# A graph network's gated projection: the first quarter split into exact parts, and the attention step ahead of it reordered

## The chip, the core and the metric

The kernel is a hand-written program for one core of a Trainium2 chip. The core has five engines that run side by side: TensorE (PE in the profile; its weight loads are shown apart as PEld), VectorE (DVE), ScalarE (ACT), GpSimd (POOL) and SyncE (SP, which here only issues DMAs). The metric is the time of one execution on the device, in microseconds (us); lower is better. Times are compared as medians of several runs.

## The reference, cut to what matters

1024 nodes with 512 features; 16 graphs of 64 nodes each attend to 256 rows of a condition of their own. Everything is float32.

```python
h = gcn(batch_norm(relu(layernorm(x))))            # dense 1024x1024 adjacency, built from 16384 edges
for i in range(4):
    h = h + attn(ln(h, ln2[i]), cond, Wq[i], Wk[i], Wv[i], Wo[i])   # 8 heads of 64
    u = ln(h, ln3[i]) @ geglu_w[i] + geglu_b[i]    # 512 -> 4096
    val, gate = split(u, 2)                        # 2048 and 2048
    h = h + (val * gelu(gate)) @ ffo_w[i] + ffo_b[i]
out = x + gcn(h) + x_in
```

The change touches the line with `geglu_w` (the gated projection) and the last two of the eight attention steps ahead of it.

## The kernel before

**Products by parts.** Most products are made of three matrix products of reduced operands: each float32 operand is split into a high part, a low part and a third one that joins both, all held in a type that TensorE takes in one pass (`float32r`, F32R). ACT makes the high part by one multiplication, DVE the low part by one `scalar_tensor_tensor`, and DVE or POOL the third. A unit of the class `Twelve` multiplies high by high and low by low into one PSUM bank (`begin`), lets ACT scale the bank, adds the product of the thirds (`end`), and an engine copies the bank out. Plain float32 matmuls are used in few places; each shows as two records in the trace.

**The gated projection.** Its output has 2048 value and 2048 gate columns, worked on in 16 column blocks of 128 (value block and gate block together), in four rounds `r` of four blocks `c`. Node and feature dimensions are halved, and the 2x2 blocks are multiplied by seven products in place of eight (a Strassen-Winograd scheme), which needs sums of blocks of the activations (`ln3S`, from `ln3T`) and of the weights. The result of a block column goes through Gelu and a product into `fT`, and by DMA to `f_dram`.

- Round 0 (`r = 0`) is done by four `Quad`s: seven plain float32 products each, of two 128x128x512 matmuls (the helper `multiply`, L304). `geglu_weights` forms the weight sums on POOL. `first` and `second` of each `Quad` (products 0 and 1) are put in between the pieces of the last attention step; `rest` does the other five and calls `fill`, which meanwhile splits the seven activation operands for the later rounds (`begin_right`, `finish_right`, `right_beside`).
- Rounds 1 to 3 are done by twelve `Chunk`s: the same seven products, each by parts, so 42 matmuls (L1121). `Chunk.sums` (POOL) forms the weight sums, `split_steps` splits them (ACT, DVE, POOL), `steps` is the order of the products.

**The attention ahead of it.** There are eight steps `g`, one for each 128 nodes (two graphs). A step makes the next step's keys and values (`keys`, `values`, units of `Twelve`, L379), mixes its own values by the probabilities (`mix`: transposes L205, `weigh` L874, then the three parts of the result, L898 to L902), makes the next step's probabilities (`scores`: L840 on PE; on DVE the row maximum L847, on ACT two exponentials L852, on DVE the reciprocal L855 and two multiplications L857, four times), and adds the projected result to `h` (`attn_out`, L912, DVE L917 and L920). After that, the rows of `h` are normalised (`moments`, `deviations`, `scaled`) and turned into `ln3T` (`ln3_turn`: four transposes, eviction by DVE L825 or ACT L827). `add_bias` (L1583) adds the last bias of the layer to `h` ahead of time.

**What sets the order.** `pin` keeps an instruction in program order among the others so marked. `with in_order(DVE)` chains every DVE instruction of a block to the one before it, in the order in which the block's text issues them; elsewhere a planner orders each queue by priority and expected readiness. Tiles of 128x1024 come from a pool of 35 `slots`; matmuls write to 8 PSUM banks.

Of the kernel before, what the change touches and what calls it, by code (L numbers as in the profile page):

```python
# [26 lines left out]
def gnn_kernel(  # L27
# [205 lines left out]
    def sums_of_b(t, b11, b12, b21, b22, t1, t2, t4, t_last=None):  # L233


        t.tensor_tensor(t1, b12, b11, OP.subtract)
        t.tensor_tensor(b12, b22, b12, OP.subtract)
        t.tensor_tensor(t2, b22, t1, OP.subtract)
        return (t_last or t).tensor_tensor(t4, b21, t2, OP.subtract)

    def sums_of_a(t, a11, a12, a21, a22, s1, s2, s4):

        t.tensor_tensor(s1, a21, a22, OP.add)  # L243
        t.tensor_tensor(a21, a11, a21, OP.subtract)
        t.tensor_tensor(s2, s1, a11, OP.subtract)
        return t.tensor_tensor(s4, a12, s2, OP.subtract)

    def halves_of(t):
        return t.rearrange("p (a b) -> p a b", a=2)

# [44 lines left out]

    def blocks_of_w(w):
        return [w[k][:, :, d * M:(d + 1) * M] for d in range(2) for k in range(2)]

    def multiply(to, left, right, cols_of, start, each=lambda ins: ins):

        for n, (l0, l1, r0, r1) in enumerate(cols_of):
            at = to if len(cols_of) == 1 else to[:, n * (r1 - r0):(n + 1) * (r1 - r0)]
            for k in range(2):
                each(nc.tensor.matmul(at, left[:, k, l0:l1], right[:, k, r0:r1],  # L304
                                      start=start and n == 0 and k == 0,
                                      stop=n == len(cols_of) - 1 and k == 1,
                                      skip_group_check=True))
# [634 lines left out]
    def order7(blk, s1, s2, s4):  # L942

        return [blk[0], blk[1], s4, blk[3], s1, s2, blk[2]]

    def load_geglu(l, r):
        return [load_w(geglu_w[l][:, r * D:(r + 1) * D], f"wval_{l}_{r}"),
                load_w(geglu_w[l][:, DFF + r * D:DFF + (r + 1) * D], f"wgate_{l}_{r}")]

    def geglu_weights(l, r, wval, wgate):  # L950
        s = slots_of(3, f"ges_{l}_{r}")
        sums_of_a(nc.gpsimd, *wval, *wgate, *s)
        return order7([*wval, *wgate], *s)

    class Quad:

        def __init__(self, l, r, c, left, right, f):
            self.n, self.c, self.f = f"{l}_{r}_{c}", c, f  # L960
            self.cv = l * 2 * DFF // P + r * KC + c
            self.left, self.right = left, right

        def product(self, i, to, start, each=lambda ins: ins):
            multiply(to, self.left[i], self.right[i],
                     [(self.c * P, (self.c + 1) * P, 0, 512)], start, each)

        def first(self):
            self.a = bank(f"ga_{self.n}")
            self.product(0, self.a, True)  # L970
            if self.c % 2 == 0:
                Quad.room = slot(f"gs1_{self.n}")
            self.s1 = Quad.room[:, self.c % 2, :]
            nc.scalar.copy(self.s1, self.a)

        def second(self):
            self.product(1, self.a, False)

        def gate(self, pre, name):
            cg = self.cv + DFF // P  # L980
            nc.scalar.activation(pre, pre, AF.Gelu, bias=gcols[:, cg:cg + 1])

        def rest(self, fill):
            n, bias = self.n, gcols[:, self.cv:self.cv + 1]
            b, c, d = (bank(f"{x}_{n}") for x in ("gb", "gc", "gd"))
            u2, u3 = (acc_tile(f"g{x}_{n}") for x in ("u2", "u3"))
            g0, g1 = (t512(f"{x}_{n}") for x in ("g0", "g1"))
            f0, f1 = self.f.of(self.c)

            def add(to, x, y):  # L990
                self.last = pin(nc.vector.tensor_tensor(to, x, y, OP.add))

            self.product(5, b, True, pin)
            add(u2, b, self.s1)
            at_once = self.c in (1, 2)
            if not at_once:
                fill()
            if not self.c:
                fill()
            self.product(6, c, True, pin)  # L1000
            add(u3, c, u2)
            if at_once:
                fill()
            fill()
            self.product(4, d, True, pin)
            add(g1, d, u3)
            self.gate(g1, n)
            fill()
            self.product(3, c, False, pin)
            add(g0, c, u2)  # L1010
            self.gate(g0, n)
            fill()
            self.product(2, d, False, pin)
            add(d, d, u2)
            pin(nc.vector.scalar_tensor_tensor(f0, self.a, bias, g0, OP.add, OP.mult))
            pin(nc.vector.scalar_tensor_tensor(f1, d, bias, g1, OP.add, OP.mult))
            self.f.store(self.c)
            fill()
            fill()

    SPLIT = (0, 5, 6, 4, 1, 3, 2)
    EARLY = (0, 1, 4, 6, 5, 3, 2)
    BESIDE = (4, 6)

    def begin_right(name, x, h, s):

        nc.scalar.mul(h.bitcast(F32R), x, INWARD / TINY)
        for k in range(2):
            more = t512(f"{name}_{k}")
            nc.scalar.mul(more, h[:, k, :], 1.0 + TINY)  # L1030
            yield
            pin(nc.vector.scalar_tensor_tensor(s.bitcast(F32R)[:, k, :], x[:, k, :], 1.0 / TINY,
                                               more, OP.mult, OP.subtract))

    def finish_right(name, x, h):

        low = slot(name)
        for k in range(2):
            yield low
            pin(nc.vector.scalar_tensor_tensor(low.bitcast(F32R)[:, k, :], x[:, k, :], 1.0 / TINY,  # L1040
                                               h[:, k, :], OP.mult, OP.subtract))
# [29 lines left out]
    class Chunk:  # L1071
# [78 lines left out]
        def steps(self, sum_next):  # L1150
# [7 lines left out]
            self.banks = {}  # L1158
            self.scale(0)
            yield  # L1160
            self.scale(5)
            yield
            s1, u2, u3 = (acc_tile(f"g{x}_{n}") for x in ("s1", "u2", "u3"))
            pin(nc.scalar.copy(s1, self.end(0)))
# [27 lines left out]
    class Gated:  # L1192
# [10 lines left out]
        def store(self, c):  # L1203
            for s in range(2):
                nc.sync.dma_start(f_dram[s, self.r * KC + c], self.tiles[c][:, s, :])

    def quads_of(l, r, left, right):
        f = Gated(l, r)
        return f, [Quad(l, r, c, left, right, f) for c in range(KC)]
# [227 lines left out]
    for l in range(L):  # L1437
# [238 lines left out]
        def all_parts():  # L1676
            for i in EARLY:
# [17 lines left out]
                for _ in flow:  # L1695
                    yield
# [275 lines left out]
```

## Time and profile before

| | |
|---|---|
| median of 3 runs | 2288.28 us (2287.64 to 2288.84) |
| profiled execution | 2287.76 us, its span 2286.0 us |
| TensorE busy | 2262.3 us, 99% of the span |
| VectorE busy | 1649.5 us, 72% |
| ScalarE busy | 1125.7 us, 49% |
| GpSimd busy | 587.2 us, 26% |

The span runs from the first to the last instruction; 1.8 us of the execution lie around it. Busy times are averages over stages that differ: the prediction reads the stage of the change by itself. The first layer's stage runs from 353.84 us (first key product of step 6) to 445.30 us (first `Chunk`), and there are four such stages, one a layer.

### The profile page before, as it was taken

To read this page: it belongs to the slowest core of one execution; us is meant where nothing else is said; L and a number is where in the kernel's file an instruction comes from. 1 tells how busy PE (TensorE), PEld (TensorE's weight loads), DVE (VectorE), ACT (ScalarE), POOL (GpSimd) and SP (SyncE) were. 2 spreads that over 40 slices of the span, in tenths; PEclk is the share of its full clock that TensorE was granted. 3 is DMA by queue.
4 is the path that set the end of the run, shared out by engine and by line. 5 is a ranking of instruction groups with operands and counts; after the bars stand their busy time and mean duration, and the time that the engine had idled before them with its cause. 6 is when DMAs were issued, how large, how long until landed. Compare 5 with 4: busy or idle time off the path is not lost. (4 is left out here: it accounts for less than half of the span.)

```text
span 2286.0 us, 34523 instructions
## 1 busy us (share of the span) xinstructions
PE 2262.3 (99%) x12496; PEld 1754.6 (77%) x12496; DVE 1649.5 (72%) x3124; ACT 1125.7 (49%) x2197; POOL 587.2 (26%) x551
## 2 busy tenths in 40 slices
PE   8999999999999999999999999999999999999999
PEld 4678887587888888488888888578888888668787
DVE  9876556999965445989976444989976444899965
ACT  7555545565354445465345444655436444556521
POOL 1121213485000002377000001368100000368301
PEclk9999999999999999999999999999999999999999
DMA  5154331234425331133534242133543332043551
GB/s 170 57 184 167 148 116 60 83 120 147 170 81 183 125 111 42 61 117 100 194 120 170 94 139 70 37 111 102 184 157 134 125 116 97 1 129 111 178 182 56
DMA packets 162545, 271.54 MB, mean 119 GB/s; under 512 B 13288, under 2 KB 70960, under 8 KB 162368
## 3 DMA queue, kind: packets, MB, share of 16 engines
q1 hardware_dynamic: 160272, 263.83, 33.7%
q0 software_dynamic: 1376, 4.30, 0.6%
q8 instruction: 103, 1.69, 0.3%
q10 hardware_dynamic: 720, 1.11, 0.1%
q14 instruction: 74, 0.61, 0.1%
HBM read 202.08 MB, written 67.11 MB: 118 GB/s over the span
## 5 line engine op out<-in xcount | busy, mean ns | idle before, releaser
L1135 ACT ACTIVATE g<-g 128x512 f32<-128x512 f32 x192 | 112.4, 586 | 153.2 <-PE g L1121 151.3
L243 POOL TENSOR_TENSOR ges<-wgate,wgate 128x1024 f32<-128x1024 f32 x4 | 9.6, 2393 | 676.6 <-DMA wgate<-in_L_gnn_geglu_w_dram 441.6
L390 ACT ACTIVATE k<-k 128x512 f32<-128x512 f32 x125 | 73.1, 586 | 194.2 <-PE k L379 194.2
L1264 PE MATMUL fx<-bs_wff,as_f 128*128 128x512 f32 x512 | 158.7, 390 | 0.0
L1264 PE MATMUL fy<-bl_wff,al_f 128*128 128x512 f32 x512 | 158.6, 390 | 0.0
L1264 PE MATMUL fy<-bh_wff,ah_f 128*128 128x512 f32 x512 | 157.8, 389 | 0.0
L321 ACT ACTIVATE ah_f<-fr 128x1024 fp32r<-128x1024 f32 x64 | 67.9, 1060 | 179.5 <-DVE al_f L322 79.8
L395 DVE COPY kT<-k 128x512 f32<-128x512 f32 x54 | 37.3, 691 | 159.5 <-PE k L379 159.1
L847 DVE TENSOR_REDUCE nmax<-sc 128x2 f32<-128x512 f32 x128 | 83.0, 679 | 88.2 <-PE sc L840 88.2
L390 ACT ACTIVATE v<-v 128x512 f32<-128x512 f32 x127 | 74.7, 588 | 137.9 <-PE v L379 137.9
L1065 POOL TENSOR_TENSOR gsa<-gha,gla 128x512 fp32r<-128x512 f32 x96 | 124.2, 1317 | 43.7 <-DVE gla L1060 43.7
L852 ACT ACTIVATE pr<-sc,nmax 128x256 f32<-128x256 f32 x256 | 118.1, 474 | 31.7 <-DVE nmax L847 31.1
L1121 PE MATMUL g<-gr,gha 128*128 128x512 f32 x384 | 120.0, 394 | 0.0
L1121 PE MATMUL g<-gr,gsa 128*128 128x512 f32 x384 | 119.8, 393 | 0.0
L1121 PE MATMUL g<-gl,gla 128*128 128x512 f32 x384 | 118.4, 389 | 0.0
L1264 PEld LDWEIGHTS fy<-bl_wff,al_f 128*128 128x128 f32 x512 | 96.1, 188 | 21.6 <-DVE bl_wff L1241 1.6
L1264 PEld LDWEIGHTS fx<-bs_wff,as_f 128*128 128x128 f32 x512 | 96.1, 188 | 21.4 <-DVE bs_wff L1245 1.7
L1264 PEld LDWEIGHTS fy<-bh_wff,ah_f 128*128 128x128 f32 x512 | 96.1, 188 | 19.9
L379 PE MATMUL v<-bh_wv,ch 128*128 128x512 f32 x384 | 106.4, 399 | 0.0
L322 DVE SCALAR_TENSOR_TENSOR al_f<-ah_f,fr 128x1024 fp32r<-128x1024 f32 x64 | 78.1, 1220 | 39.1 <-ACT ah_f L321 33.0
L379 PE MATMUL k<-ch,bh_wk 128*128 128x512 f32 x384 | 103.4, 391 | 0.0
L1312 POOL TENSOR_TENSOR as_wq<-ah_wq,al_wq 128x512 fp32r<-128x512 f32 x16 | 21.1, 1342 | 319.7 <-DVE al_wq L1310 286.2
(333 smaller groups left out, 6015.8 us busy)
## 6 DMA issues: line engine op xcount, KB each, us to landing
f_dram<-fT SPq DMA_DIRECT2D x128, 256.0 KB, 2.1
fr<-f_dram SPq DMA_DIRECT2D x64, 512.0 KB, 5.1
ch<-cond_dram SPq DMA_DIRECT2D x48, 512.0 KB, 4.8
cl<-cond_dram SPq DMA_DIRECT2D x48, 512.0 KB, 6.1
cs<-cond_dram SPq DMA_DIRECT2D x48, 512.0 KB, 7.1
wff<-in_L_gnn_ffo_w_dram SPq DMA_DIRECT2D x32, 512.0 KB, 5.5
gxa<-in_L_gnn_geglu_w_dram SPq DMA_DIRECT2D x96, 128.0 KB, 2.5
gxb<-in_L_gnn_geglu_w_dram SPq DMA_DIRECT2D x96, 128.0 KB, 2.5
```

The costliest lines, as they stand in the source:

```text
L321: nc.scalar.mul(twelve_bits(h), x, INWARD * TINY)
L322: left_parts.low = nc.vector.scalar_tensor_tensor(twelve_bits(l), h, -1.0 / TINY, x, OP.mult, OP.add)
L379: pin(nc.tensor.matmul(self.bank, twelve_bits(left[k // 2])[:, k % 2, self.c * P:(self.c + 1) * P], twelve_bits(right[k // 2])[:, k % 2, : ...
L390: nc.scalar.mul(self.bank, self.bank, 1.0 + TINY)
L395: nc.vector.tensor_copy(self.to(), self.bank)
L847: nc.vector.tensor_reduce(nmax, ps3, AX.X, OP.max, negate=True)
L852: nc.scalar.activation(pr3[:, a, :], ps3[:, a, :], AF.Exp, bias=nmax[:, a:a + 1], accum_out=tot[:, a:a + 1])
L1065: split_left.last = pin(t.tensor_tensor(s_at, h_at, l_at, OP.subtract))
L1121: pin(nc.tensor.matmul(to, self.part(i, which)[:, k, :], self.rights[i][which].bitcast(F32R)[:, k, :], start=start and k == 0, stop=stop a ...
L1135: pin(nc.scalar.mul(to, to, 1.0 + TINY))
L1264: pin(nc.tensor.matmul(to, twelve_bits(left[which][0])[:, k, b * P:(b + 1) * P], twelve_bits(right[which])[:, k, :], start=u == 0 and whic ...
L1312: nc.gpsimd.tensor_tensor(twelve_bits(s)[:, k, :], h[:, k, :], l[:, k, :], OP.subtract)
```

## The change

Round 0 is done in another way, and steps 6 and 7 are written out anew:

- The four `Quad`s and all that served them alone are gone (`geglu_weights`, `multiply`, `begin_right`, `finish_right`).
- Column blocks 0 and 1 of round 0 (`PLAIN = 2`) are done without the seven-product scheme: for each half of the nodes, a gate unit and a value unit a block, each a `Half(Twelve)` of 12 matmuls by parts. Its weights are loaded by two DMAs (`HalfWeights`) and split into parts; its activations are the split blocks 0 and 1 of `ln3T` for the first half, and 7 and 2 for the second.
- Column blocks 2 and 3 become `Chunk`s like those of the later rounds: 14 `Chunk`s a layer, not 12.
- The activation operands are split elsewhere: 0 and 1 within step 6 (third part on POOL), 7 and 2 by column halves within step 7, the sums 5, 6, 4 and 3 beside the second half's units. Operand 7, the unchanged block, is new; `ln3_last_sum` replaces it by its difference later.
- Step 6 is wholly inside one `in_order(DVE)` block, the `scores` of step 7 among it; its `attn_out` moves into step 7, as a hook of `mix` between the transposes and `weigh`. The transposes of normalised blocks move to between the keys. The bias is added by POOL alone.

```diff
+    class Half(Twelve):
...
+        def multiply(self, which, start, stop):
+            for k in range(KC):
+                right = self.right[k // 2][which]
+                pin(nc.tensor.matmul(self.bank, twelve_bits(self.left[which])[:, k, ...],
+                                     twelve_bits(right)[:, k % 2, :], ...))
+        def end(self):
+            self.multiply(2, False, True)
+            self.emit(self.bank)
...
+        take_ln3()
+        weights = HalfWeights(l)
+        load()
+        with in_order(mybir.EngineType.DVE):
+            k = keys(l, g + 1, wk)
+            k[0].begin()
...
+            ln3_turn(0, (1, 1), pin)
+            ln3_turn(1, (0, 0), pin)
+            add_bias(nc.gpsimd, *range(4))
...
+            ln3_norm(g - 2, g - 1)
...
+            oT = mix(l, g, probs, vs.pop(g), (
+                k[-1].end, lambda: split_early(0), v[0].begin,
+                lambda: split_early(1)))
+            add_bias(nc.gpsimd, g - 2, g - 1)
+            weights.split(1)
+            probs = scores(l, g + 1, qT, kTs.pop(g + 1))
+            oT = oT()
+            weights.split(0)
+            v[1].begin()
+            v[0].end()
+            ln3_turn(g - 2, (1, 1), pin)
+            v[2].begin()
+            v[1].end()
+            ln3_turn(g - 1, (0, 0), pin)
+            ln3_sums(nc.gpsimd, g - 2, g - 1)
+            sum_chunk(0)
+            v[3].begin()
+            v[2].end()
...
+        with in_order(mybir.EngineType.DVE):
+            units = half_0(0) + half_0(1)
...
+            oT = mix(l, g, probs, vs[g], (v[3].end, attn_before))
+            units[0].begin()
+            oT = oT()
+            split_late(slice(0, 2 * P))
+            long = begin_split(0, False)
+            next(long)
+            for _ in attn_out(l, g, oT, wo, pin):
+                pass
...
+            units[1].begin()
+            units[0].end()
...
+            units[2].begin()
+            units[1].end()
+            units[3].begin()
+            ln3_turn(g - 1, (1, 1), pin)
+            ln3_turn(g, (0, 0), pin)
+            units[2].end()
+            ready[0].begin_first()
+            units[3].end()
+            split_late(slice(2 * P, 4 * P))
+            ready[0].end_first()
+            ln3_sums(nc.vector, g - 1, g)
+            ln3_last_sum(nc.gpsimd, g - 3, g - 2)
+            ln3_last_sum(nc.gpsimd, g - 1, g)
...
+        units = half_1(0) + half_1(1)
+        units[0].begin()
+        fill(2)
+        units[1].begin()
+        units[0].end()
...
-        for r in range(1, R):
+        for r in range(R):
-            for c in range(KC):
+            for c in range(0 if r else PLAIN, KC):
```

More of the change, by code (lines that the diff above doesn't have):

```diff
@@ L289, in gnn_kernel @@
     left = None
[L296 to L307, printed above, removed]
     def twelve_bits(t):
@@ L940, in out_parts @@
             yield
[L942 to L1019, printed above, removed]
@@ L1770, in split_rest @@
+        for _ in range(2):
+            next(first_flow)
+        fill(2)
+        units[3].end()
+        load()
+        second = begin_split(1, False)
+        add_bias(nc.gpsimd, g - 1, g)
         def split_rest(short, behind=None):
@@ L1812, in gnn_kernel @@
                         next(before, None)
+                    elif not step:
+                        next(second)
                     next(flow)
                     if step == 1 and not before:
-                        split_rest(iter(()))
+                        for _ in second:
+                            pass
+                        sum_chunk(1)
                         load()
```

333 lines of the change are left out of this document (179 added, 154 removed).

## The prediction, made before the changed kernel was run

> **What bounds the kernel now.** I read the page's busy times first, then the busy time of each engine in the four stages of the change (a layer each; the fifth row is the first layer's `Chunk` loop, from another answer of the same view), then TensorE's waits.
>
> ```profile
> PE 2262.3 (99%) x12496; PEld 1754.6 (77%) x12496; DVE 1649.5 (72%) x3124; ACT 1125.7 (49%) x2197; POOL 587.2 (26%) x551
> core 0: us, PE busy (x) PEld busy (x) DVE busy (x) ACT busy (x) POOL busy (x), PEclk, DMA share, GB/s
> 353.84:445.30 91.46, 90.53 (x462) 55.81 (x460) 74.71 (x158) 45.02 (x86) 34.61 (x30) 1.00 0.15 50
> 880.76:972.22 91.46, 90.54 (x462) 55.83 (x460) 74.93 (x158) 45.03 (x86) 34.67 (x30) 1.00 0.15 48
> 1407.84:1499.72 91.88, 90.53 (x462) 55.82 (x460) 75.70 (x158) 45.02 (x86) 34.61 (x30) 1.00 0.16 50
> 1935.33:2026.78 91.45, 90.53 (x462) 55.81 (x460) 74.64 (x158) 45.02 (x86) 34.63 (x30) 1.00 0.15 47
> 445.30:560.00 114.70, 114.70 (x502) 93.42 (x500) 104.55 (x148) 68.84 (x118) 89.30 (x88) 1.00 0.35 111
> PE po L874 <- DVE pT L888: 1.2, 4, 0.3
> ```
>
> TensorE is the bound nearly everywhere, at full clock, and the stages are alike. So the time is TensorE's own work plus what it waits. In the `Chunk` loop it waits for nothing although DVE is busy 91% and POOL 78%: busy helpers alone do not stop it. Only a serial chain that ends later than TensorE arrives does.
>
> **TensorE's work: what goes and what comes.** The first layer's plain products and the pace of both kinds (columns of the last four rows: start, length, then how many):
>
> ```profile
> L304 PE MATMUL ga<-ln3T,wval 128*128 128x512 f32 x32 | 14.8, 595 | 0.0
> L304 PE MATMUL gd<-ln3T,ges 128*128 128x512 f32 x16 | 7.7, 604 | 0.5 <-DVE g L991 0.5
> L304 PE MATMUL gc<-ln3S,wgate 128*128 128x512 f32 x16 | 7.6, 599 | 0.1
> L304 PE MATMUL gc<-ln3T,wgate 128*128 128x512 f32 x16 | 7.5, 592 | 0.0
> L304 PE MATMUL gb<-ln3S,ges 128*128 128x512 f32 x16 | 7.5, 592 | 0.0
> L304 PE MATMUL gd<-ln3S,ges 128*128 128x512 f32 x16 | 7.5, 592 | 0.0
> 437.12 1.88 PE L304 MATMUL gb<-ln3S,ges 128*128 128x512 f32 x4
> ...
> 443.98 1.88 PE L304 MATMUL gd<-ln3T,ges 128*128 128x512 f32 x4
> 356.57 1.07 PE L379 MATMUL k<-ah_c,bh_wk 128*128 128x512 f32 x4
> ...
> 361.11 1.07 PE L379 MATMUL k<-ah_c,bh_wk 128*128 128x512 f32 x4
> 423.86 1.88 PE L304 MATMUL gc<-ln3S,wgate 128*128 128x512 f32 x4
> 426.28 1.98 PE L304 MATMUL gd<-ln3T,ges 128*128 128x512 f32 x4 [0.54 <-DVE g L991]
> 445.30 1.02 PE L1121 MATMUL g<-gr,gha 128*128 128x512 f32 x2
> ```
>
> There are 32 + 5 x 16 = 112 records, four to a product (two matmuls, two records each): 28 products a layer. Matmuls overlap, so the price is the distance of starts: 437.12 to 443.98 is four products, 1.715 us each. The matmuls by parts take (361.11 - 356.57) / 20 = 0.227 us each.
>
> - Removed: 28 x 1.715 = 48.0 us a layer.
> - Added: 2 blocks x 2 halves x 2 (gate, value) x 12 = 96 matmuls, and 2 `Chunk`s x 42 = 84; 180 x 0.227 = 40.9 us. The nearest row, the `Chunk` loop, has no lost time at 12 x 42 matmuls in about 115 us, so I take this pace for both.
> - Moved at the same count: the key, value, `scores`, `mix`, `attn_out` and turning matmuls.
>
> Net 7.1 us less a layer. Today's waits go with their code: the 12 products from 423.86 to 445.30 take 21.4 instead of 20.6, so 0.9 is lost, 0.7 of it ahead of 426.28; `weigh` loses 0.3 (the waits above); and the first pair of the first `Chunk` lasts 1.02, where 0.62 would be its pace (1.07 for four less two distances), 0.4. Together 1.6 a layer. New waits decide what is left.
>
> **The helpers' work.** DVE loses the `Quad`s' sums and products, and gains little; the rest of its rows, for all chains below:
>
> ```profile
> 353.84:445.30 91.46, 12.73 (x19) 1.00 0.15 50
> L1583 POOL TENSOR_TENSOR hall<-hall,ffb 128x512 f32<-128x512 f32 x2 | 2.8, 1402 | 10.4 <-DVE xn_ln L193 10.4
> L825 DVE TENSOR_SCALAR ln3T<-tr_ln,cols 128x128 f32<-128x128 f32 x16 | 5.7, 404 | 1.4 <-ACT ln3T L827 1.2
> L245 POOL TENSOR_TENSOR ges<-ges,wval 128x1024 f32<-128x1024 f32 x1 | 2.4, 2405 | 0.0
> L827 ACT ACTIVATE ln3T<-tr_ln,cols 128x128 f32<-128x128 f32 x16 | 6.4, 458 | 1.7 <-PE tr_ln L205 1.4 <-DVE ln3T L825 0.2
> L1060 DVE SCALAR_TENSOR_TENSOR gla<-gha,gxa 128x1024 fp32r<-128x1024 f32 x10 | 12.2, 1220 | 5.0 <-ACT gha L1059 5.0
> L1060 DVE SCALAR_TENSOR_TENSOR glb<-ghb,gxb 128x512 fp32r<-128x512 f32 x10 | 9.9, 986 | 0.0
> L1032 DVE SCALAR_TENSOR_TENSOR gr<-ln3T,gt 128x512 fp32r<-128x512 f32 x6 | 4.0, 680 | 0.0
> L857 DVE TENSOR_SCALAR pr<-pr,inv x256: 340/348/882, 168.1 to 1972.5; 128x256 f32<-128x256 f32 x128
> ```
>
> The first row is L991 alone (the additions). In the stage up to the `Chunk`s DVE loses these 12.7 us, 8 products and six bias additions at about 0.68 (what L1032 shows for 128x512), some 22 us; it gains 4 products and two weight splits of 1.22, some 5. The activation splits take 24 instructions before and after: seven operands then, eight now, but POOL makes the thirds of four and not of two. So some 58 us remain of the 64 that the stage then lasts (91.5 - 48.0 + 96 x 0.227, less waits). POOL loses four weight sums of 2.4 and gains four bias additions of 1.4 and eight thirds, of two operands and the weights, at the same 1.4: from 35 to some 42. Both shares (91%, 66%) are no higher than the `Chunk` loop's. The two weight DMAs have the size of the four they replace (512 KB each) and are issued as early, and the two more `Chunk`s' loads find the DMA engines 15% busy: hidden; without that cover a late load would hold ACT's split first, and TensorE by as much as it is late.
>
> **Where TensorE would wait: step 6 into step 7.** Today the planner orders `scores`: two maxima run first and reciprocals slip in between. In the new block DVE's chain forbids that: maximum, ACT's two exponentials, reciprocal, two multiplications, and only then the next maximum. The rows of a step where each piece is seen:
>
> ```profile
> 340.83 1.96 PE L840 MATMUL sc<-kT,qT 64*64 64x256 f32 x32
> 341.96 1.29 DVE L847 TENSOR_REDUCE nmax<-sc 128x2 f32<-128x512 f32 x2 [1.36 <-PE sc L840]
> 342.69 0.47 ACT L852 ACTIVATE pr<-sc,nmax 128x256 f32<-128x256 f32 x1 [1.14 <-DVE nmax L847]
> 343.51 0.20 ACT L852 ACTIVATION_READ_ACCUMULATOR pr<-sc,nmax 128x1 f32 x1
> 346.12 0.15 DVE L855 RECIPROCAL inv<-tot 128x2 f32<-128x2 f32 x1
> 346.31 0.61 DVE L857 TENSOR_SCALAR pr<-pr,inv 128x256 f32<-128x256 f32 x2
> 376.92 1.91 PE L205 MATMUL tr_ln<-ident,xn_ln 128*128 128x128 f32 x16
> 378.58 1.17 PE L379 MATMUL v<-bh_wv,ah_c 128*128 128x512 f32 x4
> 374.95 0.17 DVE L155 TENSOR_SCALAR v_ln<-mv_ln 128x2 f32<-128x2 f32 x1
> 377.12 1.00 DVE L193 TENSOR_SCALAR xn_ln<-hall,mv_ln,y_ln 128x512 f32<-128x512 f32 x2
> ```
>
> A round is 0.65 + 1.0 (342.69 to 343.71) + 0.15 + 0.6 + hops of 0.1 = 2.5 us; four are 10. Counted from the first score matmul, DVE starts at 1.1 and is through at 11.1. Queued behind it: the result's low and third parts (2 x 0.68), a weight split (1.22), four evictions (5.7 / 4 = 1.4), a value copy, two copies of turned probabilities and the last value copy (4 x 0.68), 6.7 in all: 17.8. `weigh` of step 7 needs that last copy. TensorE has, until then, the scores (1.9), 40 value matmuls (9.1), 24 transposes of 0.104 (2.5) and `attn_out` (2.7): 16.2. It waits 1.6, if POOL is idle. But a multiplication L857, 0.35 alone, took up to 0.88 where POOL ran; eight of them by +0.53 are 4.2, wait 5.8. POOL has the early thirds and half of the weights' beside the first half of this chain, and the nearest row for such a crowd, L1060 in the `Chunk` loop, shows +0.3 (986 against 680 alone). So some +1: I take 2.6, nearer to the idle end, since POOL's thirds cover only part of the chain; ends 1.0 (ACT and DVE overlap better than I count) and 5.8.
>
> The Trainium skill, page "SBUF — State Buffer", section "Who interferes with whom", calls the port pair that DVE and GpSimd share an exclusive lock: whoever issues second "fully blocks" for the whole instruction. By that rule the eight could each wait for a whole POOL instruction of 1.4, 11 us, and TensorE near 13; the row's 0.53 agrees with a blocking, not with that size.
>
> **Step 7 and the second half.** From the end of `weigh`, DVE has: the high part on ACT (an estimate of 0.7, from L852's 0.47 at half the width), low and third (1.4), four late splits (2.7), a `Chunk` split (1.2), two additions (1.4), statistics (an estimate of 0.9, one long and one small instruction), eleven small instructions (374.95 to 377.12, 2.2), the first scaling (0.5): 11.0. TensorE arrives at the turning after 52 matmuls, 11.8: no wait, though five splits at +0.3 to +0.5 make it up to 1.8. Then 8 transposes and 14 matmuls bring TensorE to the second half at 15.9; there ACT has evicted four tiles (12.8 to 14.4 at 0.40 each), a Gelu, a scaling and the first high part behind it (0.7 each, estimated as above): 16.5, with a hop 16.6. Wait 0.7, ends 0 and 1.8 (the late low parts of 0.7 each behind it). The sums 5, 6, 4, 3 come off DVE at 2.8, 2.8, 1.4, 1.4 against 2.7 a unit; the thirds of 4 and 3 on POOL are the tight ones: 0.5, ends 0 and 2.
>
> Sum of new waits: 2.6 + 0.7 + 0.5 = 3.8 a layer; ends 1.0 and 11.4 (5.8 + 1.8 + 1.8 + 2). Per layer: -7.1 - 1.6 + 3.8 = -4.9; four layers -20. The profiled execution, 2287.76 (span 2286.0), lies 0.5 under the median 2288.28; with the median as base the result is **2268**. The ends: 2288.3 - 4 x 7.7 = 2257, and 2288.3 + 4 x 2.7 = 2299.
>
> **Rivals.**
> - *The chains are hidden.* For it: the `Chunk` loop's full cover at DVE 91%. Against: `scores` in strict order is a chain, not a load. New waits of 1 to 2 us: 2257 to 2261, most likely 2259.
> - *The wait moves, larger.* DVE near its end value ahead of `weigh`, little else late: 6 to 8 us a layer, 2277 to 2285.
> - *The port decides (other sign).* POOL's 42 us fall on the softmax and on the late splits. At 11.4 a layer: 2299. It turns at 7.1 + 1.6 = 8.7 us of waits a layer. For it: 0.88 against 0.35. Against: TensorE loses nothing in the `Chunk` loop with POOL at 78%. The Trainium skill's lock (page "SBUF — State Buffer") speaks for it too, and would make it worse.
> - *The count gives nothing.* The new units read weights laid out otherwise and might run slower than 0.227; 0.04 more a matmul over 180 eats the 7.1: about 2288. No row speaks for it: keys and `Chunk`s, laid out differently, both run at 0.227 to 0.229.
>
> **How the numbers follow.** Forecast (waits 2 to 6 a layer, 2261 to 2277) 0.50; hidden 0.27; larger wait 0.12, a tenth of it within 0.2% of before; port 0.08; count 0.03. 0.2% is 4.6 us, about what a measurement of this kernel can tell from no change. Faster: 0.50 + 0.27 + 0.10 = 0.87; same 0.05; slower 0.08. The range 2256 to 2281 leaves out the port, the count and the worse half of the larger wait, some 0.17.
>
> **What the profile after would show.** Right: no plain products by `multiply`; 56 `Chunk`s of 42 matmuls; a layer some 5 us shorter with 7.1 less work; the one repeated wait of TensorE at `weigh` of step 7, for a copy by DVE; L857 longer than 0.35 in that step. Wrong: idle time at the turned blocks or at the first units of the second half over 2 us; a longer distance of starts in the new units; POOL busy without a break while TensorE waits for a third part.

## The result: 27 us slower, and the profile after

The changed kernel takes 2315.43 us (2314.95 to 2316.21), the one before 2288.20 beside it: ratio 1.0119, interval 1.0102 to 1.0137. Forecast was 2268. The profiled execution took 2315.27 (span 2313.5). First the busy line of the page after. Then, for the first layer, the `Chunk` loop before, up to the first product behind it; its stage ahead (91.46 us) is a row of the prediction. Then the changed kernel: the stage up to the first `Chunk` of the loop, and the loop up to the same product:

```profile
PE 2256.9 (98%) x12768; PEld 1804.2 (78%) x12768; DVE 1675.7 (72%) x3048; ACT 1163.8 (50%) x2273; POOL 704.2 (30%) x639
```

```profile
445.30:561.50 116.20, 116.17 (x506) 94.20 (x505) 105.36 (x149) 69.30 (x119) 89.30 (x88) 1.00 0.36 114
```

```profile
354.03:428.31 74.28, 69.79 (x456) 55.34 (x455) 59.42 (x112) 43.20 (x85) 38.69 (x31) 0.98 0.13 40
428.31:568.29 139.98, 135.69 (x580) 106.73 (x579) 127.43 (x176) 80.39 (x140) 111.43 (x107) 1.00 0.36 112
```

Before, the two stretches lasted 91.46 + 116.20 = 207.66 us and TensorE (first busy figure) idled 1.0. After, they last 214.26 and it idles 8.8, and the clock of the first stretch is 0.98. By the count and the old waits they should have lasted 207.66 - 7.1 - 1.6 = 199.0 us: 15.3 us a layer were lost where 3.8 were forecast. TensorE's waits after that come back in every layer (total, times, longest):

```profile
PE v L348 <- ACT v L359: 9.1, 5, 2.2
PE g L1050 <- ACT g L1064: 8.4, 4, 2.1
PE tr_ln L205 <- DVE xn_ln L193: 5.3, 4, 1.4
PE g L1050 <- POOL gs L983: 2.9, 4, 0.7
PE g L1050 <- DVE gl L1740: 2.6, 4, 0.7
PE g L936 <- DVE gr L1621: 1.6, 4, 0.4
PE g L1050 <- DVE g L1068: 1.4, 4, 0.4
PE g L1050 <- DVE gl L981: 1.2, 4, 0.3
```

Counted as the distance of starts beyond the pace, the first layer loses 4.1 in the value units (place A; 2.35 of it in one pause), 1.5 at the turned blocks, 3.7 in five waits at the second half and the first `Chunk`, 2.3 in one pause of the second `Chunk` (place D): 11.6. The rest is the clock (below) and stalls under 0.3 each. (A distance of starts beyond the pace comes out some 0.16 larger than the wait of the list, since the length of a matmul in the trace, 0.39, is more than its pace, 0.227.) `weigh` (`po`), where the forecast put its largest wait, is not among TensorE's waits.

Place A, in the timeline of the changed kernel (start, length; rows chosen by engine: DVE, POOL, ACT, TensorE, the last with the first score matmul ahead):

```profile
370.30 4.65 DVE L1621 SCALAR_TENSOR_TENSOR gr<-ln3T,gr 128x512 fp32r<-128x512 f32 x4
374.88 2.31 DVE L291 SCALAR_TENSOR_TENSOR al_gp<-ah_gp,gp 128x1024 fp32r<-128x1024 f32 x1
377.11 0.68 DVE L816 TENSOR_REDUCE nmax<-sc 128x2 f32<-128x512 f32 x1
379.08 1.94 DVE L826 TENSOR_SCALAR pr<-pr,inv 128x256 f32<-128x256 f32 x2
380.94 0.68 DVE L816 TENSOR_REDUCE nmax<-sc 128x2 f32<-128x512 f32 x1
371.24 7.10 POOL L1628 TENSOR_TENSOR gr<-gr,gt 128x512 fp32r<-128x512 f32 x4 [2.53 <-DVE gr L1621]
378.30 2.57 POOL L299 TENSOR_TENSOR as_gp<-ah_gp,al_gp 128x512 fp32r<-128x512 f32 x2
381.65 0.47 ACT L821 ACTIVATE pr<-sc,nmax 128x256 f32<-128x256 f32 x1 [2.80 <-DVE nmax L816]
382.56 0.59 ACT L359 ACTIVATE v<-v 128x512 f32<-128x512 f32 x1
373.36 1.96 PE L809 MATMUL sc<-kT,qT 64*64 64x256 f32 x32
379.94 1.08 PE L348 MATMUL v<-bl_wv,al_c 128*128 128x512 f32 x4
383.21 2.07 PE L348 MATMUL v<-bs_wv,as_c 128*128 128x512 f32 x4 [2.19 <-ACT v L359]
```

Follow it back from the last row: TensorE waits for ACT's scaling of a value unit (382.56); that stands in ACT's queue behind exponentials, which idle 2.80 for the second maximum on DVE (380.94); that follows two multiplications stretched to 1.94, after a first maximum at 377.11, which itself stood behind four low parts (4.65) and a weight split (2.31). The low parts and the split ran beside POOL's early thirds, the multiplications beside its thirds of the weights.

Place D, same view (rows chosen):

```profile
434.88 3.97 POOL L983 TENSOR_TENSOR gr<-gl,gt 128x512 fp32r<-128x512 f32 x2
438.80 2.54 POOL L994 TENSOR_TENSOR gsa<-gha,gla 128x512 fp32r<-128x512 f32 x2
442.12 2.04 POOL L1022 TENSOR_TENSOR gxa<-gxa 128x256 f32<-128x256 f32 x2
444.19 1.06 ACT L988 ACTIVATE gha<-gxa 128x1024 fp32r<-128x1024 f32 x1 [4.18 <-POOL gxa L1022]
445.62 0.59 ACT L1064 ACTIVATE g<-g 128x512 f32<-128x512 f32 x1
446.35 0.70 PE L1050 MATMUL g<-gs,gsa 128*128 128x512 f32 x2 [2.11 <-ACT g L1064]
```

TensorE waits for a scaling on ACT, which stands behind the split of the third `Chunk`; that waits 4.18 for POOL's sums, which stand behind the thirds of parts 4 and 3 and the second `Chunk`'s third.

And the clock: three neighbouring stretches of 3.41 us after place A begins (PE busy, clock, DMA share, GB/s):

```profile
379.84:383.25 3.41, 1.22 (x7) 1.00 0.00 0
383.25:386.66 3.41, 3.41 (x10) 0.50 0.00 0
386.66:390.08 3.42, 3.40 (x19) 1.00 0.01 2
```

Four such half-clock stretches stand in the changed kernel between the first layer and the output, one a layer: behind place A in layers 1 and 3 (383.2 and 1451.6 us), behind place D in layers 2 and 4 (980.6 and 2048.9). None stands in the one before.

### The profile page after: what moved, and what is told of

Read it like the earlier page. It is cut to its first block, busy times and chain, and to the rows that moved or that the text cites. A ratio compares the mean times of both kernels' runs of the same rounds, so it can differ in the third digit from the quotient of the medians.

```text
span 2313.5 us, 35383 instructions
## 1 busy us (share of the span) xinstructions
PE 2256.9 (98%) x12768; PEld 1804.2 (78%) x12768; DVE 1675.7 (72%) x3048; ACT 1163.8 (50%) x2273; POOL 704.2 (30%) x639
## 5 line engine op out<-in xcount | busy, mean ns | idle before, releaser
L1525 POOL TENSOR_TENSOR hall<-hall,ffb 128x512 f32<-128x512 f32 x32 | 42.3, 1347 | 696.4 <-DMA ffb<-in_L_gnn_ffo_b_dram 433.2
L1064 ACT ACTIVATE g<-g 128x512 f32<-128x512 f32 x224 | 131.4, 587 | 170.6 <-PE g L1050 169.3
L994 POOL TENSOR_TENSOR gsa<-gha,gla 128x512 fp32r<-128x512 f32 x112 | 142.8, 1298 | 9.7 <-issue 7.3
L1050 PE MATMUL g<-gr,gha 128*128 128x512 f32 x448 | 138.1, 389 | 0.0
L1050 PE MATMUL g<-gs,gsa 128*128 128x512 f32 x336 | 108.1, 401 | 11.3 <-ACT g L1064 8.4
L1050 PE MATMUL g<-gl,gla 128*128 128x512 f32 x336 | 106.2, 393 | 4.2 <-DVE gl L1740 2.6
L348 PE MATMUL v<-bs_wv,cs 128*128 128x512 f32 x384 | 103.8, 393 | 6.6 <-ACT v L359 6.6
L994 POOL TENSOR_TENSOR gsb<-ghb,glb 128x512 fp32r<-128x512 f32 x56 | 73.8, 1318 | 110.6 <-DVE gla L989 65.7
```

The lines of the kernel that those rows point to most:

```text
L348: pin(nc.tensor.matmul(self.bank, twelve_bits(left[k // 2])[:, k % 2, self.c * P:(self.c + 1) * P], twelve_bits(right[k // 2])[:, k % 2, : ...
L994: split_left.last = pin(t.tensor_tensor(s_at, h_at, l_at, OP.subtract))
L1050: pin(nc.tensor.matmul(to, self.part(i, which)[:, k, :], self.rights[i][which].bitcast(F32R)[:, k, :], start=start and k == 0, stop=stop a ...
L1064: pin(nc.scalar.mul(to, to, 1.0 + TINY))
L1525: t.tensor_tensor(h[nb], h[nb], ffb[0], OP.add)
```

## The experiments

Each is an edit of the changed kernel. "Windows" are half-clock stretches of 3.41 us in its trace between the first layer and the output. Where `scores` is edited, later lines are numbered 11 higher. The comments in the code below are added here.

**One suspect each.** e1 lets the next maximum go ahead of this reciprocal on DVE in the last `scores`:

```diff
...
+        for u in range(4):
+            begun.append(begin(u))      # maximum, exponentials
+            if len(begun) > ahead:      # 1 in the last scores, else 0
+                end(*begun.pop(0))      # reciprocal, multiplications
...
```

> The maximum of the next score bank goes ahead of the reciprocal of this one in the hand-written DVE order of step 6; nothing else changes. Strict-order theory (the softmax rounds of 2.5 us on DVE hold up ACT's scaling of a value bank, and TensorE behind it): TensorE's 2.2 us wait for a value bank goes, the two halves of the clock loss there go too, 3 to 5 us a layer, 2296 to 2304. Port theory (POOL stretches DVE in step 6 so far that the order does not matter): under 1 us a layer, 2312 to 2315.

2308.17, ratio 1.0084 (1.0055 to 1.0114), seven windows: between the two forecasts. 7 us gained; but the value unit still waited 9.3 us in all for ACT (9.1 in the changed kernel), now with the third maximum (381.01) held by the stretched multiplications (1.94) alone.

e2 puts the late splits and the first `Chunk`'s split behind the last normalisation:

```diff
-            split_late(slice(0, 2 * P))
-            long = begin_split(0, False)
-            next(long)
             for _ in attn_out(l, g, oT, wo, pin):
...
+            split_late(slice(0, 2 * P))
+            long = begin_split(0, False)
+            next(long)
             units[1].begin()
```

> In step 7 the late splits and the first chunk's split go behind the normalisation in DVE's order, not ahead of it. Chain theory (TensorE waits 1.5 us at the turned blocks because these splits stand ahead of the normalisation): that wait goes and 1 to 1.5 us a layer with it, 2309 to 2312. Full-DVE theory (DVE has no idle time from there to the second half, so what is taken from one wait returns at the next): the wait at the turned blocks goes, the waits at the second half grow by as much, 2314 to 2317.

2327.20, ratio 1.0168 (1.0138 to 1.0197), six windows: above both forecasts. The wait at the turned blocks went; in its place TensorE waits 8.6 us (2.1 a layer) for the first `Chunk`'s low part, and the waits for the lows of parts 5 and 6 grew from 2.6 to 6.5 in all. So these splits are late at either place.

e3 makes the thirds of parts 4 and 3 on DVE, e4 the thirds of the early parts:

```diff
-    ALONE = (5, 6)
+    ALONE = (5, 6, 4, 3)
```

```diff
-            for _ in split_right(i, ln3T[0][i], pool=True):
+            for _ in split_right(i, ln3T[0][i]):
```

> The thirds of the operands 4 and 3 are made by DVE, not POOL (four DVE instructions of 0.69 more, four POOL instructions less, which took 7.2 us in the first layer). POOL-backlog theory (the 2.3 us wait in the second chunk is ACT's split standing behind POOL's late weight sums): that wait goes, and the one for the third part; 2 to 4 us a layer, 2299 to 2307. Full-DVE theory: the 2.8 us of DVE work return as waits for its additions and splits, 2313 to 2320.

> The early thirds of operands 0 and 1 are made by DVE, not POOL: four DVE instructions more, four POOL instructions and four ACT passes less, in step 6. Port theory: the four early low parts shrink from 4.65 us together to 2.7, the first normalising multiplications from 1.94 to 0.6, the weight split from 2.3 to 1.2, so the 2.7 us added are paid back; the wait for the value bank stays or shrinks, 2305 to 2316. Load theory (DVE instructions count at their lone length and POOL's neighbours do not matter): the softmax ends 2.7 us later, TensorE waits that much longer in each layer, 2324 to 2328.

e3: 2308.78, ratio 1.0087 (1.0058 to 1.0116), three windows, between its forecasts: the pause at D fell from 2.3 to 0.7, and waits for the lows of the parts 5, 6, 4 and 3 rose from 3.8 (2.6 and 1.2 in the list above) to 9.2 us in all. e4: 2309.72, ratio 1.0091 (1.0062 to 1.0121), six windows, within the port theory's range: the 1.94 became 1.20, and the strict order now held the exponentials: a wait of 2.0 in the next value unit. No one of the four explained 27 us. At place A, e1 and e4 each took away one of two causes that covered each other, which e5 tests.

**Causes together.** e5 is e1 with e4; e6 adds to it a later issue of the third `Chunk`'s split on ACT; e7 is e5 with e3; e8 is e6 with DVE's `ln3_sums` between the lows and the thirds of the second `split_late`. The edits of e6 and e8:

```diff
-                    if not the_last:
+                    if not the_last and before is not first_flow:
                         split_rest(short)
...
                     next(flow)
+                    if before is first_flow and not step:
+                        split_rest(short)
```

```diff
-            split_late(slice(2 * P, 4 * P))
+            split_late(slice(2 * P, 4 * P), lambda: ln3_sums(nc.vector, g - 1, g))
             ready[0].end_first()
-            ln3_sums(nc.vector, g - 1, g)
```

> In step 7 both edits at once: the next maximum ahead of this reciprocal on the vector engine, and the thirds of the two early right parts on the vector engine instead of POOL. In the traces of the two edits alone the 2.4 us wait of the value unit per layer only changed its last cause (a weight third on POOL stretching the divisions to 1.94 us a pair, or the exponentials behind the strict softmax order), so neither removed it. Theory 'two causes in one place, and half-clock windows': the wait goes only here, 2.4 us a layer and the clock window that follows it, so about 2294 us (2290 to 2298), with one half-clock window a layer left, at the second chunk (around 444 us and one per layer after). Rival 'the gains merely add' (7.1 + 5.7 off 2315.4, no clock effect): 2301 to 2304. Rival 'the wait moves to the next late thing': 2306 to 2312, and a pause of 2 us still shows in the value units around 381 us.

> As the one before, and the split of the third chunk's weights is issued on the scalar engine one step later, behind the second chunk's copy and scaling instead of ahead of them (its input comes from POOL's sums, which stand behind the thirds of parts 4 and 3). Theory 'the pause at the second chunk is that order on the scalar engine': 2.25 us a layer go and with them the half-clock window after each, so 9 + 7 off the kernel before this one: about 2278 us (2274 to 2283), granted clock near 1.0. Rival 'the pause goes but the clock has no price': 9 off, 2285 to 2294. Rival 'POOL itself is late': the third chunk then waits for its split and the time stays within 3 us of the kernel before.

> As the first of this group, with the thirds of parts 4 and 3 on the vector engine too (POOL holds no thirds of right parts any more). Theory 'POOL's backlog makes the pause at the second chunk, and the clock follows the pause': the pause shrinks from 2.25 to about 0.7 us, the vector engine's later thirds cost 1 us a layer (as in the trace with that edit alone), and the window goes: 2281 to 2287 us. Rival 'gains add, no clock': 2294 to 2297. Rival 'vector engine full': 2298 or more.

> As the second of this group, with the sums of the second half's right parts put between the lows and the thirds of the late split on the vector engine. Theory 'the second half starts late because parts 5 and 6 wait for sums that stand last in the vector engine's order': the waits of 0.8 and 0.9 us at the start of the late parts shrink, 1 to 1.5 us a layer, so 4 to 6 below the kernel before it: 2273 to 2279. Rival 'the thirds of parts 7 and 2 are then late instead': equal to it within 2 us, or up to 4 above.

e5: 2298.33, ratio 1.0047 (1.0031 to 1.0064), no window, though the pause at D stayed: place A is gone, as the first theory said, though the last transposes of the softmax now wait 1.6 for DVE; the time is just above the forecast. e6: 2297.55, 1.0041 (1.0027 to 1.0056), no window: of 2.3 at D, 1.5 and 0.6 stayed; the third theory, POOL itself is late. e7: 2291.04, 1.0015 (1.0005 to 1.0025), two windows in the layers, between its forecasts: POOL's backlog taken away gave 7 us. e8: 2301.19, 1.0059 (1.0042 to 1.0075), no window: a miss for its theory; as the rival said, the thirds of the late parts were late instead, 1.8 a layer.

**Order or amount on DVE?** From e7: e9 has both lows of a late part ahead of both thirds; e10 puts the second weight split behind the turned block's eviction; e11 has both, e12 both with part 3's thirds on POOL.

```diff
-            for k in range(2):
-                yield low
+            yield low
+            for k in range(2):
                 pin(nc.vector.scalar_tensor_tensor(low.bitcast(F32R)[:, k, :], x[:, k, :], 1.0 / TINY,
...
+            yield low
+            for k in range(2):
                 pin(nc.vector.scalar_tensor_tensor(s.bitcast(F32R)[:, k, :], h[:, k, :], -TINY,
```

```diff
-            weights.split(0)
             v[1].begin()
             v[0].end()
             ln3_turn(g - 2, (1, 1), pin)
+            weights.split(0)
```

> The three edits that gave 2291 (next maximum ahead of this reciprocal; early thirds, and the thirds of parts 4 and 3, on the vector engine), and in the late right parts both lows stand ahead of both thirds, since the first two products of a part need the lows and the third product comes later. In the trace of 2291 the chunks' starts wait for these lows 0.8, 0.5 and 1.6 us a layer with the vector engine busy from 418.6 us on. Theory 'the order low, third, low, third keeps the lows late': 1 to 2 us a layer go, 2283 to 2287. Rival 'the vector engine's sum of work is the bound there': the thirds are late instead, 2289 to 2293.

> The three edits that gave 2291, and the second split of the half blocks' weights is issued behind the eviction of the first turned block instead of ahead of it. In the trace of 2291 the last transposes of the softmax wait 1.6 us a layer for that eviction, which stands behind the weights' lows of 1.22 us on the vector engine. Theory 'that order makes the wait': 1.0 to 1.4 us a layer go, 2285 to 2288. Rival 'the weights' thirds on POOL come 1.2 us later and the half units wait for them': equal within 1.5 us.

> The last two edits together. If both theories hold: 2277 to 2282, below the kernel before (2288). If either wait only moves: 2284 to 2288.

> As the one before, with the thirds of part 3 alone back on POOL (1.3 us a layer off the vector engine, some 4 us onto POOL ahead of the second chunk's third). Theory 'vector engine is the bound at the start of the late parts': 1 to 3 us below the one before. Theory 'POOL's backlog makes the second chunk's pause': the pause there comes back in part (over 1 us a layer at the scaling of the second chunk), 3 to 8 us above it.

e9: 2287.72, ratio 0.9996 (0.9986 to 1.0005), no window: equal to the kernel before, the best complete version found, and between its two forecasts. e10: 2294.55, 1.0022 (1.0013 to 1.0032), four windows, worse than e7 and above both forecasts. The wait of 1.6 a layer at the transposes went and the normalisation's grew from 2.6 to 9.7 us in all. One row of e9 and one of e10, the same operation, shows how:

```profile
399.56 1.21 DVE L1000 SCALAR_TENSOR_TENSOR gla<-gha,gxa 128x1024 fp32r<-128x1024 f32 x1
```

```profile
399.10 2.31 DVE L1000 SCALAR_TENSOR_TENSOR gla<-gha,gxa 128x1024 fp32r<-128x1024 f32 x1
397.55 1.07 POOL L1033 TENSOR_TENSOR gy<-gxb,gxa 128x256 f32<-128x256 f32 x1
398.58 1.74 POOL L1503 TENSOR_TENSOR ln3T<-ln3T,ln3T 128x512 f32<-128x512 f32 x1
```

In e10 this low, and the late splits ahead of it, ran beside POOL's sums; in e9 POOL was idle then. e11: 2291.15, 1.0007 (0.9998 to 1.0017), three windows, above both forecasts: the normalisation's 9.7 stayed, and 7.1 in all for the second `Chunk`'s low. e12: 2296.17, 1.0029 (1.0019 to 1.0040), with 2.3 a layer back at D, as the theory of POOL's backlog said.

**The clock, and the last of the order.** e13 is e9 with the second `Chunk`'s low ahead of the last thirds; e14 is e13 with e10's edit, and `next(long)` behind the last normalisation. e15 (on e1) and e16 (on the changed kernel) compute twelve matmuls a layer twice, inside the two pauses. The edits of e13, e14, and of e15 and e16:

```diff
+                if not before:
+                    next(second)
                 for _ in parts:
                     pass
...
-                    elif not step:
-                        next(second)
```

```diff
             long = begin_split(0, False)
-            next(long)
             for _ in attn_out(l, g, oT, wo, pin):
...
+            next(long)
             units[1].begin()
```

```diff
-            v[2].begin()
+            v[2].begin(True)      # its first two products twice
...
+            for _ in range(1 + (i == 4 and self.n.endswith("_0_3"))):
                 self.multiply(i, 0, to, True, False)
                 self.multiply(i, 1, to, False, True)
```

> The kernel that equalled the one before (2287.7), with the second chunk's low of 1.21 us ahead of the last two thirds (2.26 us) on the vector engine instead of behind them. In that kernel's trace the second chunk's start waits 1.9 us a layer for this low. Theory 'order': 1.0 to 1.9 us a layer go, 2280 to 2284, below the kernel before. Rival 'sum of work': the thirds of part 3 or POOL's third of the second chunk are late instead, 2286 to 2289.

> As the one before it here, with the second split of the half blocks' weights behind the first turned block's eviction, and the first chunk's low (2.31 us while POOL works, 1.21 alone) behind the last normalisation instead of ahead of it. The weights' split alone had moved a wait of 1.6 us from the softmax's transposes to the normalisation (0.8 to 2.6 us), where splits of 2.4 us in place of 1.3 stood beside POOL's sums. Theory 'POOL's stretch ahead of the normalisation': with one of the stretched operations out of the way 1 to 1.5 us a layer go: 4 to 6 below the one before. Rival 'the first chunk's low is then late': equal or up to 8 above.

> The kernel with the next maximum ahead of this reciprocal (2308.2, seven half-clock windows), and in it the first two products of one value unit (8 matmuls) and of one product of the second chunk (4 matmuls) are computed twice into the same bank, in the two places where TensorE pauses 2.3 to 2.4 us a layer: 48 matmuls of 0.227 us more in the program, 10.9 us of work, and the wait behind each pause ends when it did. Theory 'the pause makes the window, and the window costs 1.7 us': all seven windows go, 12 us less for more work: 2295 to 2298. Rival 'the window has no cost of its own': 2307 to 2310. Rival 'the added work delays the scaling or what follows': 2312 to 2320.

> The changed kernel (2315.4, four half-clock windows) with the same twelve matmuls a layer computed twice. Theory 'pause makes window': the four windows go, 6.8 us less: 2307 to 2310. Rival 'no cost of its own': 2314 to 2317. Rival 'added work delays': 2319 to 2327.

e13: 2291.01, 1.0010 (1.0001 to 1.0019), above both forecasts; e14: 2290.80, 1.0009 (1.0000 to 1.0019), equal to e13, as its rival said. Both are no better than e9: in e13 one wait of 3.4 a layer for a scaling-and-sum on DVE replaced the 1.9, with three half-clock stretches, two of them two windows long. e15: 2302.61, 1.0059 (1.0044 to 1.0075): 5.6 us less than e1 with 10.9 us more of TensorE's work, and no window. (The intervals of the two ratios overlap; the single times, 2302.35 to 2304.29 and 2307.19 to 2309.15, do not.) The same stretches of place D in e1 and in e15 (busy PE, PEld, DVE, ACT, POOL; clock):

```profile
440.18:443.59 3.41, 1.33 (x6) 0.81 (x5) 1.62 (x2) 2.38 (x4) 1.72 (x3) 1.00 0.00 0
443.59:447.00 3.41, 3.41 (x9) 2.64 (x9) 3.14 (x6) 2.18 (x5) 3.40 (x4) 0.50 0.28 106
```

```profile
440.18:443.59 3.41, 2.19 (x10) 1.53 (x10) 1.68 (x2) 2.33 (x4) 1.79 (x3) 1.00 0.00 0
443.59:447.00 3.41, 3.41 (x15) 2.47 (x15) 3.08 (x5) 2.24 (x5) 3.34 (x4) 1.00 0.26 99
```

So the pause makes the window, and the window costs time: the wait ends at 443.4 in both, and at 449 us e15 is 1.25 ahead. It is less than the 12 us expected, since of those 1.25 the first layer gives 1.0 back by 565 us, mostly in stalls of about 0.1 at the third products, which follow ACT's scalings; e1, further behind, did not meet them. e16: 2317.97, 1.0124 (1.0108 to 1.0139), 2.5 slower than the changed kernel with no window. The rival that a window costs nothing is not refuted by this run, since other waits grew: the next value unit's scaling moved behind the last exponentials on ACT (388.44 where it had been 385.12), and waits of 1.1 and 1.8 a layer followed. It tells nothing on the window's price.

**Less split work.** e17 (on e9) and e18 (on the changed kernel) leave out the thirds of the right parts, and with them ACT's passes for those on POOL: the third products read the high part again, so TensorE's work is the same.

```diff
-            h, low, third = rights[i]
+            h, low, _ = rights[i]          # rights[i] = [h, low, h]
...
-                Chunk.rights[i] = high, next(flow), mid
+                Chunk.rights[i] = high, next(flow), high
```

> The kernel that equalled the one before (2287.7), with the thirds of the right parts of the gated projection's products left out (the third products read the high part again, so TensorE's work is the same): per layer 16 operations of 0.6 us less on the vector engine, 10 us, around the last attention step and the chunks' start. Theory 'sum of work on the vector engine': the waits of 1.6, 0.9, 0.6, 1.9, 0.6 and 0.7 us a layer in that trace mostly go, 4 to 6 us a layer: 2264 to 2272, which is where the count of products alone puts the change. Rival 'chain of waits': the transposes, the normalisation and the chunk's low keep their places, at most 2 us a layer go: 2280 to 2287.

> The changed kernel (2315.4) with the same thirds left out, those on POOL too. Theory 'sum of work': the pause at the second chunk (2.3 us a layer, POOL's backlog) goes, that in the value units (2.4 us) at least shrinks, and with them the windows: 2278 to 2290. Rival 'the strict order of the softmax alone makes the pause in the value units': that pause stays at 2 us or more and 2290 to 2300 results.

e17: 2263.38, ratio 0.9889 (0.9872 to 0.9905), just below its first forecast. e18: 2274.67, 0.9935 (0.9919 to 0.9952), 41 us below the changed kernel and below both of its forecasts. Neither has a window. e17's list of TensorE's waits begins so (total, times, longest); no wait in it occurs four times, once a layer, any more:

```profile
PE edges L467 <- DVE high L453: 3.8, 1, 3.8
PE pc L471 <- DMA prow<-in_L_gnn_bn_b_dram: 3.3, 1, 3.3
PE begun_k L335 <- DVE v_deg L155: 2.2, 1, 2.2
PE edges L467 <- DVE outside L463: 1.5, 1, 1.5
PE k L348 <- ACT k L359: 1.5, 1, 1.5
PE cs L611 <- DVE lo L576: 0.7, 1, 0.7
```

Place A in e18 (rows chosen: DVE, then TensorE):

```profile
370.59 2.48 DVE L1620 SCALAR_TENSOR_TENSOR gr<-ln3T,gr 128x512 fp32r<-128x512 f32 x4
373.38 1.23 DVE L291 SCALAR_TENSOR_TENSOR al_gp<-ah_gp,gp 128x1024 fp32r<-128x1024 f32 x1 [0.30 <-ACT ah_gp L290]
374.78 0.69 DVE L816 TENSOR_REDUCE nmax<-sc 128x2 f32<-128x512 f32 x1 [0.18 <-PE sc L809]
376.56 0.17 DVE L824 RECIPROCAL inv<-tot 128x2 f32<-128x2 f32 x1 [1.09 <-ACT pr L821]
373.65 1.96 PE L809 MATMUL sc<-kT,qT 64*64 64x256 f32 x32
379.76 1.08 PE L348 MATMUL v<-bl_wv,al_c 128*128 128x512 f32 x4
380.68 1.07 PE L348 MATMUL v<-bs_wv,as_c 128*128 128x512 f32 x4
```

The strict order is still there (the reciprocal idles 1.09 for ACT), and TensorE no longer pauses: the first maximum starts at 374.78, when the scores are ready, and not at 377.11. My theory from e1, that the strict order makes the pause, falls: from an early start it makes none. In e4 it made one with a late first maximum (376.80) and multiplications of 1.20; how much of either it takes was not separated.

The kernel before makes thirds as well, so 2263 is no price of this change against an equal kernel. It shows that most of what the count promises is there once DVE and POOL are out of the way: 26 of the 35 us that 7.1 and 1.6 a layer make. Fewer instructions and a shorter queue ahead of each chain went together here; which of the two decides was not separated.

## Why the prediction was wrong

- **Right: TensorE's count.** The new units run at 0.227, and e17, with hardly a wait, takes 26 us less than the kernel before beside it (2289.60). That is 6.6 of the 8.7 a layer that the count and the old waits make; in the first layer of e17 no distance of starts is more than 0.3 above the pace, and the missing 2.1 was not followed further. The rival that the count gives nothing falls.
- **Wrong: "Counted from the first score matmul, DVE starts at 1.1".** This is the step that failed. I summed DVE's work by stage and found room (58 of 64 us), and began the softmax with a free DVE. In the strict order four lows and a weight split stand ahead of the first maximum, and my sum had no term for them. Beside POOL's thirds they take 4.65 and 2.31, and the maximum starts 3.75 us after the first score matmul (377.11 against 373.36). In e18, without those thirds, the same operations take 2.48 and 1.23, and it starts at 1.1. So that queue alone would have been through in time; as POOL stretches it, it was not.
- **Right for its rows, but put on too few: "some +1" for the port.** For the eight multiplications it was near: the first pair took 1.94 and the other three 0.62 each, 1.3 more than four undisturbed pairs. What it left out is the stretch ahead of the softmax: by the rows of e18, 2.2 on the four lows and 1.1 on the weight split, 3.3 more.
- **Wrong place: `weigh` of step 7.** The forecast followed DVE's queue to its last copy and found 1.6 to 2.6 there. The first to wait was ACT's queue: a value unit's scaling behind exponentials, TensorE behind that. `weigh` waited nothing.
- **Mis-sized: "Wait 0.7, ends 0 and 1.8" at the second half.** The waits there sum to 3.7, five links and not one: the late lows (L1621), the lows of parts 5 and 6 (L1740), those of parts 4 and 3 (L981), their thirds (L983), the first scaling-and-sum (L1068).
- **Missed: the second `Chunk`.** For the thirds on POOL I took 0.5, counting only those who read them. Behind them in POOL's queue stood the next `Chunk`'s sums, behind these a split on ACT, behind that the scaling: 2.3.
- **Turned blocks: 1.5**, within the end written (1.8), not the 0 taken.
- **Missed: the clock.** No term allowed for it; one window a layer, in which half the clock takes at most half of 3.41, 1.7 us.
- **The rival of the other sign** had the direction, and its turning point (8.7 us of waits a layer) was passed by 6.6. Its chance of 0.08 came from the `Chunk` loop's full cover, which says nothing of a stage where each engine waits for the next.

The Trainium skill, page "SBUF — State Buffer", section "Who interferes with whom", was cited for the shared port as an exclusive lock. The trace agrees that DVE's operations take longer while POOL works, but not with the size worked out there: in the rows shown no single operation got longer by more than one POOL instruction (1.1 us on the weight split; 1.3 on the pair of multiplications).

## What to carry to other kernels

When a change shortens the bounding engine's stretch, do not ask whether the helpers' busy share still fits: list, for the first instruction of each chain, what stands ahead of it on its own queue, with the stretched durations, and follow the wait through every queue it holds up. A work item moved to an idle engine is priced by all that stands behind it there. Where two causes cover each other, edits of one alone show little: take both away, or take the work away, before judging the order.

## What the hardware showed that was not expected

A pause well under one 3.41 us window halves TensorE's clock for the whole next window. I took the windows of the changed kernel and of e1 to e18 between 350 and 2100 us, and in each what TensorE's busy time leaves of 3.41 us (the profile models the ends of matmuls, so this is no exact idle time). All 28 windows with 2.06 us or more idle were followed by a half-clock one; of those between 1.66 and 2.06, 13 of 34; of those below, none. The least idle window that was still followed by half the clock is one of e7:

```profile
428.08:431.49 3.41, 1.74 (x7) 0.86 (x6) 3.41 (x7) 0.45 (x2) 0.00 (x0) 1.00 0.30 101
```

So the same pause of 2.1 to 2.3 us at place D counts or not by where it falls. In e1 it was followed by a half-clock window in every layer; in e5 it fell across two windows in three of the four layers (in the fourth 1.73 us fell into one), and no half-clock window followed. The Trainium skill, page "TensorE: Matmul & The Clock Gate", section "Part 1: The HAM clock gate (the "warmup" mystery)", says that the half rate follows an idle window of some 3.4 us; the window's length agrees, but here some 60% of it idle was always enough, and about half was at times. What decides between 1.66 and 2.06 us is not shown. All this makes gains of single edits uneven: e1 removed waits and had seven windows where the changed kernel had four.
